# A convolution in nine full taps, and an output projection moved to two later steps, in a two-layer kernel

## The chip, the cores and the metric

One Trainium2 chip, of which the kernel uses one core. The metric is the device time in microseconds (us) of one execution. Each core has a matrix engine (TensorE, PE in the profile), a vector engine (VectorE, DVE), a scalar engine for activation functions (ScalarE, ACT), a general engine (GpSimd, POOL), and a queue (SyncE, SP) that starts transfers. They run side by side, each through its own list of instructions in order, and wait for one another through semaphores.

## The reference, cut to what matters

The input x has 8 images of 128 channels and 128 x 128 points, in float32. Two layers follow each other; the change is in the second alone.

```python
y = conv(x1, conv_w, 3x3, padding 1) + conv_b          # 128 -> 128 channels
seq = y.reshape(B*H*W, 8, 16)                          # each point: 8 tokens of 16
xz = seq @ in_proj.T                                   # to 2 x 32
xi, z = split(xz)
xc = silu(causal conv of 4 over tokens(xi) + b)
dt, Bm, Cm = split(xc @ x_proj.T)                      # 1, 16, 16
dt = softplus(dt * dt_w + dt_b)
h = exp(dt * A) * h + dt * Bm * xc                     # scan over the 8 tokens
ym = (sum over the 16 states of h * Cm) + D * xc
out = (ym * silu(z)) @ out_proj.T
xp = silu(group_norm(out, 4 groups) * gn_w + gn_b)
result = x1 + xp
```

x1 is the output of layer 0 (a dilated convolution, a Fourier stage and a gate), which lies in DRAM.

## The kernel before, in words

Layer 0 ends at about 2950 us and layer 1 fills the rest. Layer 1 goes through 256 blocks, each of 4 rows of one image (512 points): 32 blocks an image, 8 images. Several blocks are in work at once: while block i goes through its scan, block i+3 has its convolution, block i+2 its projection to xc and z, block i+1 its dt, B and C, and block i-1 its last sums and its output projection.

The order is written by hand: under a manual schedule every engine takes its instructions in program order. For each i the program runs `step(i, s)` for s = 2 to 11, and then `seam(i)`. The scan has 16 parts for a block (`s`, 8 tokens by 2 pairs of groups of channels); the names of its operations are:

- `spreads`: TensorE spreads dt*A into the PSUM tile da and dt*xc into ups, for part s+1 and s+2. A tile is 128 partitions x 1024 numbers, made by four matmuls of 16 rows, each shown as two records.
- `exps`: ScalarE takes the exponential of da, in place.
- `inject`: VectorE multiplies ups by B into h. `decay`: VectorE multiplies da by the h of the token before. `add`: VectorE (in parts 4, 7 and 10 GpSimd) adds both.
- `weigh`: GpSimd multiplies h by C into hc. `collect`: TensorE sums hc over the states into the PSUM tile yps. `last_decay`: VectorE, for parts 14 and 15.
- `skip`: TensorE adds D times xc to yps. `ends_sum` and `ends_inputs` begin yps; `gated` multiplies it by silu(z) into ym.
- `project_out`: TensorE projects ym with m_o into the PSUM tile pm, 8 matmuls in two halves of 4; at the end ScalarE copies pm to xr. `keep` later takes the statistics of xr and sends it to DRAM.

[...]da has two buffers (`pair`, shared with `project_x` and `project_z`), ups one, yps one, and pm one. The single pm serves in turn for the convolution, the transpose of its result (`turn`), dt (`project_dt`), B and C (`project_bc`), the output projection, and the sums of the norm. Each use waits until ScalarE has copied the last one out:

```python
    p_u = ctx.enter_context(tc.tile_pool(name="l1_pu", bufs=1, space=PSUM))
    p_a = ctx.enter_context(tc.tile_pool(name="l1_pa", bufs=2, space=PSUM))
    p_m = ctx.enter_context(tc.tile_pool(name="l1_pm", bufs=1, space=PSUM))
    p_y = ctx.enter_context(tc.tile_pool(name="l1_py", bufs=1, space=PSUM))
```

The convolution (`conv`, by `_conv_taps`) is not issued at once but in pieces between the other work: 9 taps, each in two halves of 2 rows (254 or 256 columns), 18 matmuls in all. `CONV` and the `taps` calls of `seam` say how many are issued where. In step 5 `project_bc(i + 1, 1)` is followed at once by the first half of `project_out(i - 1)`; in step 6 the second half and then `skip` follow.

When an image is through, `norm_of` makes its scale and bias, and its 32 blocks are finished one by one beside the next image's: `last_load` (step 8) fetches a block, `last_act` (seam) has ScalarE apply the norm and Silu, `last_sum` (step 9) adds x1 on GpSimd and stores.

In the changed kernel the lines below the first edit stand two lines higher.

Of the kernel before, what the change touches and what calls it, by code (L numbers as in the profile page):

```python
# [116 lines left out]
def _taps(dil):  # L117

    t = [(ky, kx) for ky in range(3) for kx in range(3)]
    t.remove((1, 1))  # L120
    return [(ky * 3 + kx, (ky - 1) * dil, (kx - 1) * dil) for ky, kx in [(1, 1)] + t]


def _conv_taps(nc, outs, wt, srcs, base, r, dil, k0=0, k1=9, parts=1):

    taps = _taps(dil)
    for k in range(k0, k1):
        n, rows = k // parts, 4 // parts  # L130
        t, dy, dx = taps[n]
        a, b = max(0, -(r + dy)), min(4, H - (r + dy))
        a, b = max(a, k % parts * rows), min(b, (k % parts + 1) * rows)
        wa, wb = max(0, -dx), min(W, W - dx)
        for out, src in zip(outs, srcs):
            nc.tensor.matmul(  # L136
                out[:, a:b, wa:wb], wt[:, t, :],
                src[:, r + dy + a - base:r + dy + b - base, wa + dx:wb + dx],
                start=(k == 0), stop=(k == parts * len(taps) - 1), skip_group_check=(parts > 1),
            )  # L140


# [203 lines left out]
def layer1(ctx, tc, x1, w1, c1, out):  # L346
# [12 lines left out]
    nc = tc.nc  # L359
# [5 lines left out]
    wt = const.tile([P, W1_N], F32, name="l1_wt")  # L365
# [7 lines left out]
    def wf(name):  # L373
        at, n = W1[name]
        return wt[:, at:at + n]

    convw = wf("conv_w").rearrange("p (t c) -> p t c", c=C)
# [15 lines left out]
    taps = cf("taps").rearrange("p (k l) -> p k l", l=L)  # L393
    w_k = wf("conv1d_w").rearrange("p (k d) -> p k d", d=DI)
    with tc.tile_pool(name="l1_prep", bufs=2) as prep:
# [18 lines left out]
        for hf in range(NH):  # L414
            for l in range(L):
                k = hf * L + l
# [28 lines left out]
    blocks = [(b, r) for b in range(B) for r in range(0, H, RB)]  # L445
# [6 lines left out]
    def live(i):  # L452
        return 0 <= i < nb
# [13 lines left out]
    def conv(i, k0, k1):  # L467
        d = st8[i]
        if k0 == 0:
            d["pm"] = misc()  # L470
        xin, lo = d["xin"]
        _conv_taps(nc, [d["pm"]], convw, [xin], lo, blocks[i][1], 1, k0, k1, 2)
        if k1 == 18:
            y = wk1.tile([P, RB, W], F32, name="y")
            nc.scalar.activation(y, d["pm"], AF.Identity, bias=wf("conv_b"))
            d["y"] = y
# [40 lines left out]
    def project_bc(i, hf):  # L517
        d, pool = st8[i], wk2 if hf else wk1
        ps = misc().rearrange("p a b -> p (a b)")
        nc.tensor.matmul(ps, m_bcf, d["xc"][:, hf, :], start=True, stop=True)  # L520
        d["bc", hf] = pool.tile([P, N], F32, name=f"bc{hf}")
        nc.scalar.copy(d["bc", hf], ps)  # L522
# [10 lines left out]
    def lay_states(i, hf, k):  # L533

        d, name = st8[i], ("bb", "cc")[k]
        v = wk2.tile([P, LP, N], F32, name=name)
        for lp in range(LP):
            at = (k * LP + lp) * DS
            nc.sync.dma_start(
                v[:, lp, :], d["bc", hf][at:at + DS, :].unsqueeze(1).broadcast_to([DS, 8, N]))  # L540
        d[name, hf] = v
# [76 lines left out]
    def collect(i, t):  # L618

        d = st8[i]  # L620
        for g in range(NG):
            nc.tensor.matmul(  # L622
                d["yps"][g * DI:(g + 1) * DI], gather[:, t % LP, :], d["hc", GP * t + g // GP][:, g % GP],
                start=False, stop=(t in (3, 6)), skip_group_check=True)

    def skip(i, hf):
        d = st8[i]
        nc.tensor.matmul(d["yps"], m_d, d["xc"][:, hf, :], start=False, stop=False, skip_group_check=True)  # L628
# [6 lines left out]
    def project_out(i, k0, k1):  # L635
        d = st8[i]
        if k0 == 0:
            d["pm"] = misc()
        for k in range(k0, k1):
            j, hf = k // NH, k % NH  # L640
            nc.tensor.matmul(  # L641
                d["pm"][:, j, :], d["ym", hf][:, j * C:(j + 1) * C], m_of[:, hf, :],
                start=(hf == 0), stop=(hf == NH - 1))
        if k1 == RB * NH:
            d["xr"] = wk2.tile([P, RB, W], F32, name="xr")
            nc.scalar.copy(d["xr"], d["pm"])
# [33 lines left out]
    fin = {}  # L680
# [9 lines left out]
    def last_act():  # L690
        b, r, sc, bi, v, res = fin["active"] = fin.pop("loaded")
        nc.scalar.activation(v, v, AF.Silu, bias=bi, scale=sc)
# [3 lines left out]
        nc.gpsimd.tensor_add(res, res, v)  # L696
        nc.sync.dma_start(out[b, :, r:r + RB, :], res)

    CONV = {8: (0, 4), 9: (4, 6), 10: (6, 8), 11: (8, 11)}

    def step(i, s):

        now, nxt = live(i), live(i + 1)
        if s == 2:
            if live(i + 4):
                load(i + 4)
            if live(i - 2) and blocks[i - 2][1] + RB == H:
                norm_of(blocks[i - 2][0])
        spreads([(i, s + 1)], [(i, s + 2)])
        exps(i, s + 1)  # L710

        if s == 2:
            if nxt:
                project_dt(i + 1, 0)
            if live(i - 1):
                collect(i - 1, 7)
        elif s == 3:
            if live(i - 1):
                collect(i - 1, 6)
                skip(i - 1, 1)  # L720
            if nxt:
                project_bc(i + 1, 0)
        elif s == 4 and nxt:
            project_dt(i + 1, 1)
        elif s == 5:
            if now:
                ends_sum(i, 0)
            if nxt:
                project_bc(i + 1, 1)
            if live(i - 1):  # L730
                project_out(i - 1, 0, 4)
        elif s == 6:
            if live(i - 1):
                project_out(i - 1, 4, 8)
            if now:
                skip(i, 0)
        elif s == 7 and now:
            collect(i, 1)
        elif s == 9 and now:
            collect(i, 2)  # L740
        elif s == 11 and now:
            collect(i, 3)
        if s in CONV and live(i + 3):
            conv(i + 3, *CONV[s])

        if now:
            decay(i, s)
            if s != 4:
                add(i, s)
            inject(i, s + 2)  # L750
            if s == 5:
                ends_inputs(i, 0)
            if s == 11:
                gated(i, 0)
        if s == 3 and live(i - 1):
            gated(i - 1, 1)

        if now:
            if s == 2:
                end_products(i, 0)  # L760
            else:
                weigh(i, s - 1, (s - 1) // GP)
            if s == 4:
                add(i, s)
            if s == 7:
                end_products(i, 1)
        if s in (3, 4) and nxt:
            inputs(i + 1, s - 3)
        if s == 9 and "active" in fin:
            last_sum()  # L770

        if s == 3 and now:
            lay_states(i, 1, 1)
        elif s == 6 and nxt:
            lay_du(i + 1, 0)
            lay_states(i + 1, 0, 0)
        elif s == 8 and tails:
            last_load()
        elif s == 10 and nxt:
            lay_states(i + 1, 0, 1)  # L780

    def seam(i):


        now, nxt = live(i), live(i + 1)

        def taps(k0, k1):
            if live(i + 3):
                conv(i + 3, k0, k1)

        spreads([(i, 13)], [(i + 1, 0)])
        exps(i, 13)
        if now:
            ends_sum(i, 1)
            decay(i, 12)
            add(i, 12)
            weigh(i, 11, 5)
            weigh(i, 12, 7)
        if nxt:
            lay_states(i + 1, 1, 0)  # L800
        if live(i + 2):
            project_x(i + 2)
        if "loaded" in fin:
            last_act()
        taps(11, 12)
        if now:
            decay(i, 13)
            add(i, 13)
            weigh(i, 13, 7)
        inject(i + 1, 0)  # L810
        if live(i + 2):
            project_z(i + 2)
        spreads([(i, 14)], [(i + 1, 1)])
        exps(i, 14)
        if now:
            ends_inputs(i, 1)
        inject(i + 1, 1)
        taps(12, 15)
        spreads([(i, 15)], [(i + 1, 2)])
        exps(i, 15)  # L820
        if live(i - 1):
            keep(i - 1)
        inject(i + 1, 2)
        if now:
            collect(i, 4)
            last_decay(i, 14)
        taps(15, 18)
        if now:
            weigh(i, 12, 6)
            last_decay(i, 15)  # L830
        spreads([(i + 1, 2)], [(i + 1, 3)])
        exps(i + 1, 2)
        inject(i + 1, 3)
        if now:
            collect(i, 5)
            weigh(i, 13, 6)
        if live(i + 3):
            turn(i + 3)
        if nxt:
            lay_du(i + 1, 1)  # L840
# [95 lines left out]
```

## Time and profile before

The time is 16181.67 us, the median of 3 runs (16174.1 to 16187.9). The profiled execution took 16182.42 us.

| | busy us | share of the span |
|---|---|---|
| TensorE, matmuls | 15146.6 | 94% |
| TensorE, weight loads (beside the matmuls) | 6663.1 | 41% |
| VectorE | 12959.8 | 80% |
| GpSimd | 12024.3 | 74% |
| ScalarE | 8098.5 | 50% |

The page gives, for each group of instructions, the source line, the engine, what it writes and reads, how often it ran, how long it was busy in all and how long one takes; after the last bar stands how long the engine was idle just before it, and what ended most of that idle. In a list of waits each row has the total, the number and the longest. A row of windows has, for a stretch of time, the busy time of each engine, then the clock that TensorE was granted (1.00 is full speed), the share of the transfer engines and GB/s. In a timeline each row has the start, the time, the engine, the line and the operation, the number of instructions merged, and in brackets the idle before.

TensorE's mean granted clock in this execution is 0.967.

### The profile page before, as it was taken

What the parts mean: (1) busy time and instruction counts of PE and PEld (TensorE: products, weight loads), DVE (VectorE), ACT (ScalarE), POOL (GpSimd) and SP (SyncE); (2) the same over time, 40 slices, a digit from 0 to 9 for tenths busy, and PEclk for the clock granted to TensorE, in tenths of its full rate; (3) what the DMA queues carried; (4) which work ended last, traced back from release to release, by engine and by line L of the source; (5) the groups of instructions that cost most, each with busy time, mean ns of one, the idle gap of its engine ahead of it and who ended that gap; (6) DMA issues with size and microseconds to landing.
All of it is one profiled execution on the core that took longest, in us unless ns stands there. A gap on an engine that the chain in (4) does not pass through costs nothing.

```text
span 16180.6 us, 210804 instructions
## 1 busy us (share of the span) xinstructions
PE 15146.6 (94%) x76456; PEld 6663.1 (41%) x76456; DVE 12959.8 (80%) x13691; ACT 8098.5 (50%) x8726; POOL 12024.3 (74%) x5892
## 2 busy tenths in 40 slices
PE   9989898999999999999999999999999999999996
PEld 4546455533333333333333333333333343333332
DVE  1515233799989999999999999999999999999995
ACT  1222212455555555555555555555555555555553
POOL 0101101588889898898898988988899889888996
PEclk9999999999999999999999999999999999999997
DMA  2322222465566666666666666666666666666665
GB/s 77 86 78 76 74 72 79 100 117 114 117 119 132 132 132 131 128 134 129 131 132 129 134 127 132 130 131 129 131 131 131 132 131 131 130 130 130 132 134 134
DMA packets 1075791, 1933.19 MB, mean 119 GB/s; under 512 B 123968, under 2 KB 255040, under 8 KB 1058368
## 3 DMA queue, kind: packets, MB, share of 16 engines
q1 hardware_dynamic: 1001472, 1850.17, 53.7%
q10 hardware_dynamic: 73280, 69.54, 1.5%
q8 instruction: 607, 9.95, 0.2%
q14 instruction: 432, 3.54, 0.1%
HBM read 375.71 MB, written 201.33 MB: 36 GB/s over the span
## 4 chain that ended last, share of the span: by engine, by line
PE 65%; DVE 14%; issue 8%; ACT 8%; POOL 3%; DMA 2%; SPq 0%; ACTq 0%; DVEq 0%; POOLq 0%
PE da L556 16%; PE yps L622 8%; PE pm L136 7%; PE cps L136 6%; PE pm L641 4%; DVE h L571 4%; DVE da L587 4%; PE yps L628 3%; PE ups L556 3%; PE da L492 3%; ACT da L561 3%; DVE h L595 2%; ACT L561 2%; DVE hc L606 2%; PE pm L508 2%
## 5 line engine op out<-in xcount | busy, mean ns | idle before, releaser
L601 POOL TENSOR_TENSOR hc<-h,cc 128x1024 f32<-128x1024 f32 x3584 | 8366.3, 2361 | 608.3 <-DVE h L595 572.7
L561 ACT ACTIVATE da<-da 128x1024 f32<-128x1024 f32 x3584 | 3612.6, 1008 | 4299.9 <-PE ups L556 2359.3
L571 DVE TENSOR_TENSOR h<-ups,bb 128x1024 f32<-128x1024 f32 x3584 | 4370.6, 1219 | 1037.2 <-PE ups L556 768.3
L556 PE MATMUL da<-du,m_a 16*128 16x512 f32 x14336 | 4145.1, 655 | 30.6 <-DVE hc L606 6.6
L556 PE MATMUL ups<-du,m_u 16*128 16x512 f32 x14336 | 4168.7, 654 | 0.7 <-DVE h L571 0.7
L595 DVE TENSOR_TENSOR h<-da,h 128x1024 f32<-128x1024 f32 x2304 | 2821.3, 1225 | 79.1
L587 DVE TENSOR_TENSOR da<-da,h 128x1024 f32<-128x1024 f32 x2304 | 2819.6, 1224 | 4.8 <-issue 1.1
L136 PE MATMUL pm<-xin,l_wt 128*128 128x254 f32 (+2 forms) x9216 | 2444.3, 398 | 5.9 <-DMA l_wt<-w 4.5
L593 POOL TENSOR_TENSOR h<-ah,h 128x1024 f32<-128x1024 f32 x768 | 1812.2, 2360 | 649.1 <-DVE ah L585 571.4
L136 PEld LDWEIGHTS pm<-xin,l_wt 128*128 128x128 f32 x9216 | 1637.9, 191 | 1501.6 <-issue 1353.7
L622 PE MATMUL yps<-hc,l_ct 128*32 128x512 f32 x14336 | 1945.6, 615 | 1.3 <-POOL hc L601 1.2
L556 PEld LDWEIGHTS da<-du,m_a 16*128 16x128 f32 x14336 | 1085.2, 185 | 1919.0 <-issue 968.2
L274 POOL TENSOR_TENSOR xr<-xr,sq 128x512 f32<-128x512 f32 x128 | 160.4, 1265 | 1654.8 <-ACT sq L273 1614.8
L556 PEld LDWEIGHTS ups<-du,m_u 16*128 16x128 f32 x14336 | 1105.7, 185 | 198.0 <-DVE h L571 122.5
L641 PE MATMUL pm<-m_o,ym 128*128 128x128 f32 x4096 | 715.3, 328 | 382.8 <-ACT bc L522 382.2
L136 PE MATMUL cps<-xin,l_wt 128*64 128x500 f32 (+2 forms) x4608 | 1024.5, 583 | 38.7 <-issue 30.3
L224 DVE COPY fT<-tps 128x512 f32<-128x512 f32 x128 | 88.5, 692 | 1180.0 <-PE tps L223 1180.0
L561 ACT ACT_TABLE_LOAD x774 | 993.0, 1283 | 16.8 <-PE ups L556 0.7
L641 PEld LDWEIGHTS pm<-m_o,ym 128*128 128x128 f32 x4096 | 604.4, 227 | 836.8 <-ACT bc L522 592.5
L585 DVE TENSOR_TENSOR ah<-da,h 128x1024 f32<-128x1024 f32 x768 | 932.4, 1214 | 0.0
L340 POOL TENSOR_TENSOR og<-og,xg 128x512 f32<-128x512 f32 x128 | 164.3, 1284 | 968.5 <-ACT og L339 831.7
L622 PEld LDWEIGHTS yps<-hc,l_ct 128*32 128x32 f32 x14336 | 284.3, 108 | 1392.0 <-issue 1054.2
(150 smaller groups left out, 15907.7 us busy)
## 6 DMA issues: line engine op xcount, KB each, us to landing
bb<-bc SPq DMA_DIRECT2D x2048, 256.0 KB
cc<-bc SPq DMA_DIRECT2D x2048, 256.0 KB
du<-dt SPq DMA_DIRECT2D x2048, 64.0 KB
du<-u SPq DMA_DIRECT2D x2048, 64.0 KB
xin<-x SPq DMA_DIRECT2D x112, 640.0 KB
xin<-x SPq DMA_DIRECT2D x48, 1408.0 KB
gn<-xr SPq DMA_DIRECT2D x256, 256.0 KB
v<-gn SPq DMA_DIRECT2D x256, 256.0 KB
```

What stands on the lines that cost most here:

```text
L136: nc.tensor.matmul(out[:, a:b, wa:wb], wt[:, t, :], src[:, r + dy + a - base:r + dy + b - base, wa + dx:wb + dx], start=(k == 0), stop=(k ...
L492: nc.tensor.matmul(ps[:, hf], m_xh[:, hf, :], d["yT"], start=True, stop=True)
L556: nc.tensor.matmul(o, w, v, start=True, stop=True)
L561: nc.scalar.activation(da, da, AF.Exp)
L571: nc.vector.tensor_mul(h, d["ups", s], state_row(i, "bb", s // GP))
L585: nc.vector.tensor_mul(d["ah"], da, before)
L587: nc.vector.tensor_mul(da, da, before)
L593: nc.gpsimd.tensor_add(h, d["ah"], h)
L595: nc.vector.tensor_add(h, d["da", s], h)
L601: nc.gpsimd.tensor_mul(hc, d["h", s], state_row(i, "cc", t))
L622: nc.tensor.matmul(d["yps"][g * DI:(g + 1) * DI], gather[:, t % LP, :], d["hc", GP * t + g // GP][:, g % GP], start=False, stop=(t in (3, ...
L641: nc.tensor.matmul(d["pm"][:, j, :], d["ym", hf][:, j * C:(j + 1) * C], m_of[:, hf, :], start=(hf == 0), stop=(hf == NH - 1))
```

## The change

Three edits, all in layer 1:

1. The convolution is issued as 9 full taps of 4 rows (508 or 512 columns) instead of 18 halves. Before, steps 8, 9, 10, 11 had 2, 1, 1 and 1.5 taps and the three places of the seam 0.5, 1.5 and 1.5; now the steps have 1, 1, 1 and 2, and the seam 1, 2 and 1. The seam's first group stands ahead of `project_x` instead of behind it.
2. `skip` (D times x) comes first in step 6. The first half of the output projection goes from step 5 to step 6, behind it; the second half from step 6 to step 8, ahead of the convolution's first tap. Nothing stands any more between B and C's projection in step 5 and the spreads of step 6.
3. In the seam, `last_act` (the norm's Silu) comes ahead of `project_x` and so ahead of the Silu of xc.

They are meant to shorten TensorE's waits for pm and for da, and to halve the convolution's instructions. The instructions of VectorE, GpSimd and the transfer queue stay in their order; ScalarE's copy of xr comes two exponentials later. The core of the diff:

```diff
-def _conv_taps(nc, outs, wt, srcs, base, r, dil, k0=0, k1=9, parts=1):
+def _conv_taps(nc, outs, wt, srcs, base, r, dil, k0=0, k1=9):
...
-    for k in range(k0, k1):
-        n, rows = k // parts, 4 // parts
+    for n in range(k0, k1):
         t, dy, dx = taps[n]
         a, b = max(0, -(r + dy)), min(4, H - (r + dy))
-        a, b = max(a, k % parts * rows), min(b, (k % parts + 1) * rows)
...
-                start=(k == 0), stop=(k == parts * len(taps) - 1), skip_group_check=(parts > 1),
+                start=(n == 0), stop=(n == len(taps) - 1),
...
-    CONV = {8: (0, 4), 9: (4, 6), 10: (6, 8), 11: (8, 11)}
+    CONV = {8: (0, 1), 9: (1, 2), 10: (2, 3), 11: (3, 5)}
...
             if nxt:
                 project_bc(i + 1, 1)
+        elif s == 6:
+            if now:
+                skip(i, 0)
             if live(i - 1):
                 project_out(i - 1, 0, 4)
-        elif s == 6:
-            if live(i - 1):
-                project_out(i - 1, 4, 8)
-            if now:
-                skip(i, 0)
         elif s == 7 and now:
             collect(i, 1)
+        elif s == 8 and live(i - 1):
+            project_out(i - 1, 4, 8)
         elif s == 9 and now:
             collect(i, 2)
...
             lay_states(i + 1, 1, 0)
+        taps(5, 6)
+        if "loaded" in fin:
+            last_act()
         if live(i + 2):
             project_x(i + 2)
-        if "loaded" in fin:
-            last_act()
-        taps(11, 12)
...
-        taps(12, 15)
+        taps(6, 8)
...
-        taps(15, 18)
+        taps(8, 9)
```

More of the change, by code (lines that the diff above doesn't have):

```diff
@@ L471, in conv @@
         xin, lo = d["xin"]
-        _conv_taps(nc, [d["pm"]], convw, [xin], lo, blocks[i][1], 1, k0, k1, 2)
-        if k1 == 18:
+        _conv_taps(nc, [d["pm"]], convw, [xin], lo, blocks[i][1], 1, k0, k1)
+        if k1 == 9:
             y = wk1.tile([P, RB, W], F32, name="y")
```

## The prediction

> **What bounds the kernel now.** I read the page first, then the waits, then steady-state windows, then one block's timeline.
>
> The page's busy line and the list of waits:
>
> ```profile
> PE 15146.6 (94%) x76456; PEld 6663.1 (41%) x76456; DVE 12959.8 (80%) x13691; ACT 8098.5 (50%) x8726; POOL 12024.3 (74%) x5892
> ```
>
> ```profile
> PE pm L641 <- ACT bc L522: 382.2, 254, 1.5
> ...
> PE da L492 <- DVE h L595: 188.4, 253, 0.7
> ```
>
> TensorE (PE) is fullest, and two waits strike it once in each of the 256 blocks: 1.50 us before the output projection (L641), which wants the single PSUM buffer pm while ScalarE still copies bc out of it, and 0.75 us before x's projection (L492).
>
> The windows: two whole blocks, then 3.4 us slices around the 1.50 us wait in the slow block (three slices) and in the fast one (three):
>
> ```profile
> 8906.70:8956.35 49.65, 47.25 (x249) 19.42 (x248) 46.51 (x43) 28.86 (x30) 45.68 (x23) 1.00 0.67 142
> 10026.00:10077.30 51.30, 48.90 (x253) 20.43 (x248) 46.54 (x43) 28.89 (x31) 45.27 (x23) 0.97 0.64 135
> 10036.10:10039.50 3.40, 3.40 (x13) 1.27 (x12) 3.37 (x4) 3.35 (x4) 2.88 (x2) 1.00 0.03 8
> 10039.50:10042.90 3.40, 1.90 (x13) 1.28 (x16) 3.36 (x4) 1.80 (x3) 3.40 (x3) 1.00 0.00 0
> 10042.90:10046.30 3.40, 3.40 (x17) 2.21 (x10) 2.58 (x3) 1.15 (x2) 1.55 (x1) 0.51 0.05 19
> 8916.50:8919.90 3.40, 3.40 (x18) 1.21 (x18) 3.40 (x4) 2.44 (x3) 3.02 (x2) 1.00 0.91 158
> 8919.90:8923.30 3.40, 2.50 (x10) 0.67 (x4) 3.37 (x4) 3.36 (x5) 2.88 (x3) 1.00 0.17 25
> 8923.30:8926.70 3.40, 2.79 (x21) 1.91 (x22) 3.04 (x4) 1.08 (x3) 3.40 (x2) 1.00 0.00 0
> ```
>
> Blocks come in kinds. The fast one takes 49.65 us at clock 1.00. In the slow one, the slice holding the whole wait has PE busy only 1.90 of 3.40 us, and the next slice runs at half clock (0.51). In the fast block the same wait is cut by the edge of two slices (2.50 and 2.79 busy) and the clock stays. ScalarE's y (L475) starts from 3204.4 to 15877.7, 250 times: 12673.3/249 = 50.90 us per block on average. So half clock costs 50.90 - 49.65 = 1.25 us a block, and the wait itself comes on top.
>
> The fast block's TensorE, ScalarE and VectorE timelines at the places that matter:
>
> ```profile
> 8921.38 1.02 PE L520 MATMUL pm<-xc,m_bc 128*128 128x512 f32 x2
> 8923.91 1.16 PE L641 MATMUL pm<-m_o,ym 128*128 128x128 f32 x8 [1.50 <-ACT bc L522]
> ...
> 8926.07 1.16 PE L641 MATMUL pm<-m_o,ym 128*128 128x128 f32 x8
> 8927.06 1.02 PE L628 MATMUL yps<-xc,m_d 128*128 128x512 f32 x2
> ...
> 8931.61 1.99 PE L136 MATMUL pm<-xin,l_wt 128*128 128x256 f32 x8
> ...
> 8946.65 1.98 PE L492 MATMUL da<-yT,m_x 128*128 128x512 f32 x4 [0.75 <-DVE h L595]
> 8948.47 0.59 PE L136 MATMUL pm<-xin,l_wt 128*128 128x254 f32 x2
> ```
>
> ```profile
> 8922.34 1.01 ACT L561 ACTIVATE da<-da 128x1024 f32<-128x1024 f32 x1
> 8923.26 0.59 ACT L522 COPY bc<-pm 128x512 f32<-128x512 f32 x1
> ```
>
> ```profile
> 8926.26 1.23 DVE L571 TENSOR_TENSOR h<-ups,bb 128x1024 f32<-128x1024 f32 x1 [0.31 <-PE ups L556]
> 8929.28 1.23 DVE L571 TENSOR_TENSOR h<-ups,bb 128x1024 f32<-128x1024 f32 x1 [0.67 <-PE ups L556]
> ```
>
> VectorE is busy 46.51 of 49.65 us and idles in two places: 0.31 + 0.67 us just after PE's 1.50 us wait, and 0.80 + 0.73 + 0.16 us in the seam. Elsewhere it runs without gaps (one of 0.15), so PE's time counts only where VectorE then waits for ups. GpSimd (45.68 busy) idles the other 4.0 us and is not the limit.
>
> [...]
>
> **The change, part by part.** PE times are from the fast block, 8900 taken off.
>
> Nine full taps for eighteen half taps. A float32 matmul shows as two records. Eight half-tap records take 8933.53 - 8931.61 = 1.92 us, six take 1.48, so each further one costs 0.22 or less, against a 0.19 us weight load beside it: the loads are hidden already. A full 512-column record steps at 0.43 us (the two of L628), twice that. So 36 x 0.213 = 18 x 0.427 = 7.7 us a block: gain 0, though half the instructions go. The groups stay seven; what changes is their size: step 8 loses a tap (-0.85), step 11 gains half (+0.43), the seam has 1 + 2 + 1 taps for 0.5 + 1.5 + 1.5.
>
> Output projection out of step 5. After bc (L520, from 21.38) PE goes straight to step 6. Its da buffer is free since 21.7 (VectorE's add of step 5), its ups buffer when inject(7) ends at 22.84. So the spreads run 22.34 to 23.94, D times x 23.94 to 24.9, then L641's first half to 25.9; bc's copy ended at 23.85, so pm is free. The ups for step 8 are done at 24.0 and VectorE's inject(8) starts at 25.86, back to back, instead of 26.26; the ups for 9 follow at 28.2, and inject(9) starts at about 28.25 instead of 29.28. VectorE gains **1.03 us** here and both idle gaps are gone.
>
> Second half in step 8, a new wait. The convolution's first tap needs pm, which ScalarE must first copy into xr. PE: spreads to 30.55, L641 (8 records, 1.05) to 31.6. ScalarE's exp ends at 31.3, so the copy runs from 31.74 for 0.585 and the tap starts at about 32.37: PE idles 0.8 us (bounds: 0.6 with no hand-over time, 1.5 as for bc now). Queued behind are one tap (1.06) and step 9's spreads, ready at 34.5; VectorE wants them at 35.3. The idle is hidden, with 0.8 us to spare, because step 8 has one tap less.
>
> Seam. add(12) is done 1.03 earlier, at 45.55. PE: ends_sum to 45.1, the new tap to 46.07 (it fills what was the 0.75 wait), x's projection to 47.9, z's to 49.15, spreads 50.3. Before, spreads ended at 51.30: 1.0 kept. Two taps instead of one and a half then take 0.43: inject(2) of the next block is 0.7 earlier. The last group is 0.43 shorter but PE must wait for last_decay(14), on VectorE, so next block's first spreads start at 55.78 against 56.49. Kept: **0.71 us a block**. The Silu of the norm now fills ScalarE's 1.53 us wait for L492; z's Silu starts when PE gives it, and the exp after it has slack: 0.
>
> Clock. The largest PE idle left inside one 3.4 us window is the 0.8 us of step 8; the slices with 2.50 and 2.79 us busy (0.6 to 0.9 idle) did not lose the clock. So the half-rate slices go: **1.25 us a block** saved.
>
> Sum: 0.71 + 1.25 = 1.96 us a block, 48.94 a block. From block 3 to 255 (253 blocks): 1.96 x 253 = 496 us, 16182 - 496 = 15686. Layer 0 and the tail are untouched.
>
> **The rivals.**
> - Forecast, 48.9 us a block: 15686. Chance 0.62.
> - Clock kept, but the new step-8 wait or the longer seam group takes back the 0.71. For: the new wait stands in a stretch (steps 8 to 11) where VectorE has no gaps, so any ups that comes late costs at once. Against: the 0.8 us of spare. 16182 - 1.25 x 253 = 15866. Chance 0.15.
> - Half rate stays, brought on by the idle in step 8, next to spreads that PE does piecemeal while waiting for VectorE. Against: 0.8 us is little over half of 1.50. 16182 - 0.71 x 253 = 16002. Chance 0.10.
> - Better: the spreads' waits for VectorE shrink too, VectorE nears its 46.5 plus one gap of 1.5: 48.0 to 48.3 a block, about 15520. Chance 0.06.
> - Slower: each block now meets a half-rate window, where at present about half do, at 15 x 3.413 = 51.2 a block: 16182 + 0.3 x 253 = 16258. For: today's slow blocks hold 51.27, so that the wait meets the same place of the next window. Against: the long wait is gone, and 48.94 plus 1.6 = 50.5 would not lock in. Chance 0.07.
>
> **How the numbers follow.** The predicted time is the first case. The range from 15510 to 15950 takes in the first, second and fourth (0.83), and with them a hand schedule off by 0.3 us a block or so, and the new wait's upper bound of 1.5 us (0.7 beyond the 0.8, less than the spare); the third and fifth (0.17) are left out. Faster by over 0.2%: the first four less some of the third's upper side, 0.91; same: 0.02; slower 0.07.
>
> **What would show it.** Right: PE's wait of L641 for bc gone; a wait of about 0.8 us of the convolution for the xr copy in step 8; no wait of L492 for VectorE; PEclk near 1.00 from 3000 to 15900; no idle of VectorE after step 5; about 48.9 us between starts of y; the convolution's records half as many and twice as long, its total busy time the same. Wrong: PEclk staying at 0.97, a step-8 wait over 1.6 us, or VectorE idling longer in the seam than 1.7 us.

## The result, and the profile after

The changed kernel takes 15807.6 us (median of 4 runs, 15803.33 to 15808.82), the one before in the same comparison 16184.78 us. The ratio is 0.9766, 95% interval 0.975 to 0.9783: 377 us, 2.3% faster. The forecast was 15686 us, a gain of 496 us; the result lies inside its range.

The page's busy line and two of its groups, and from the list of waits the one that the change brought:

```profile
PE 15002.4 (95%) x71848; PEld 5732.8 (36%) x71848; DVE 12932.0 (82%) x13691; ACT 8126.9 (51%) x8726; POOL 12028.2 (76%) x5892
...
L569 DVE TENSOR_TENSOR h<-ups,bb 128x1024 f32<-128x1024 f32 x3584 | 4364.3, 1218 | 688.1 <-PE ups L554 307.2
...
L134 PE MATMUL pm<-xin,l_wt 128*128 128x508 f32 (+1 forms) x4608 | 2409.4, 623 | 176.0 <-ACT xr L644 170.2
```

```profile
PE pm L134 <- ACT xr L644: 170.2, 252, 0.7
```

The waits of 382.2 us (output projection for bc) and 188.4 us (x's projection for VectorE) are gone from the list. In place of the first stands the convolution's wait for the copy into xr, 0.7 us in each block. The second was not saved but moved: TensorE still waits for VectorE in the seam, now ahead of spreads (L554) and of z's projection (L499), for 134.6 + 76.0 = 210.6 us in all.

```profile
PE da L554 <- DVE hc L604: 134.6, 255, 1.5
...
PE da L499 <- DVE h L593: 76.0, 253, 0.5
```

The convolution has half the records and each takes longer, with 2409.4 us busy in all against 2444.3. VectorE's idle before the product with ups fell from 1037.2 to 688.1 us.

Windows of the changed kernel: one whole block, the 3.4 us slice with the new wait, the slice after it, and then nearly all of layer 1 (columns as before; the one after the POOL count is the clock):

```profile
8879.10:8928.32 49.22, 47.73 (x233) 16.31 (x233) 46.42 (x43) 29.00 (x31) 45.72 (x23) 1.00 0.63 131
8901.40:8904.80 3.40, 2.72 (x21) 1.59 (x17) 3.37 (x4) 1.60 (x2) 3.40 (x2) 1.00 0.81 90
8904.80:8908.20 3.40, 3.40 (x19) 1.04 (x20) 3.37 (x4) 1.01 (x1) 3.40 (x3) 1.00 0.91 203
```

```profile
4500.00:15400.00 10900.00, 10555.74 (x50777) 3609.56 (x50776) 10258.11 (x9331) 6412.43 (x6634) 10082.38 (x4851) 1.00 0.64 135
```

The slice with the wait has PE busy 2.72 of 3.40 us, and the next one keeps clock 1.00; so does layer 1 as a whole. Nearly the same stretch of the kernel before, 4500 to 15800, stood at 0.97. The 49.65, 51.27 and longer blocks have, but for those about the end of an image, become one kind: 49.22 us. The start of y runs from 3199.9 to 15495.3 us, 250 times, which makes 12295.4/249 = 49.38 us a block on average, against 50.90.

The changed kernel's timelines at the same places, TensorE first, then VectorE's idle times in one block:

```profile
8902.94 1.16 PE L639 MATMUL pm<-m_o,ym 128*128 128x128 f32 x8
8904.78 1.12 PE L134 MATMUL pm<-xin,l_wt 128*128 128x512 f32 x2 [0.68 <-ACT xr L644]
...
8920.53 1.13 PE L499 MATMUL da<-yT,m_z 64*128 64x512 f32 x4 [0.30 <-DVE h L593]
```

```profile
8880.32 1.23 DVE L569 TENSOR_TENSOR h<-ups,bb 128x1024 f32<-128x1024 f32 x1 [0.16 <-PE ups L554]
8900.60 1.22 DVE L569 TENSOR_TENSOR h<-ups,bb 128x1024 f32<-128x1024 f32 x1 [0.16 <-PE ups L554]
8910.24 1.22 DVE L569 TENSOR_TENSOR h<-ups,bb 128x1024 f32<-128x1024 f32 x1 [0.22 <-issue]
8922.92 1.22 DVE L569 TENSOR_TENSOR h<-ups,bb 128x1024 f32<-128x1024 f32 x1 [0.80 <-PE ups L554]
8925.90 1.22 DVE L569 TENSOR_TENSOR h<-ups,bb 128x1024 f32<-128x1024 f32 x1 [1.15 <-issue]
```

The kernel before, in step 10 and in the seam:

```profile
8938.84 1.23 DVE L571 TENSOR_TENSOR h<-ups,bb 128x1024 f32<-128x1024 f32 x1 [0.15 <-issue]
8951.52 1.22 DVE L571 TENSOR_TENSOR h<-ups,bb 128x1024 f32<-128x1024 f32 x1 [0.80 <-PE ups L556]
8954.08 1.22 DVE L571 TENSOR_TENSOR h<-ups,bb 128x1024 f32<-128x1024 f32 x1 [0.73 <-issue]
```

Read down these brackets of after against those of before. After step 5 VectorE idled 0.31 + 0.67 us; now 0.16. In step 10 it was 0.15; now 0.22. In the seam it was 0.80 + 0.73; now 0.80 + 1.15. So 0.8 us is won behind step 5, and half of it is lost in the seam before the third product of the next block (8925.90), which follows the middle group of taps.

### The profile page after: what moved, and what is told of

Its sections match the earlier page's. It is cut to its first block, busy times and chain, and to the rows that moved or that the text cites. A ratio compares the mean times of both kernels' runs of the same rounds, so it can differ in the third digit from the quotient of the medians.

```text
span 15801.5 us, 201588 instructions
## 1 busy us (share of the span) xinstructions
PE 15002.4 (95%) x71848; PEld 5732.8 (36%) x71848; DVE 12932.0 (82%) x13691; ACT 8126.9 (51%) x8726; POOL 12028.2 (76%) x5892
## 4 chain that ended last, share of the span: by engine, by line
PE 71%; DVE 17%; issue 5%; ACT 4%; DMA 2%; POOL 1%; SPq 0%; ACTq 0%; DVEq 0%; POOLq 0%
PE da L554 18%; PE yps L620 8%; PE ups L554 7%; PE pm L134 7%; PE cps L134 6%; DVE da L585 6%; DVE h L593 4%; DVE h L569 4%; PE yps L626 3%; PE pm L506 3%; PE pm L639 3%; PE pm L518 3%; DVE hc L604 2%; PE da L499 2%; PE yps L610 2%
## 5 line engine op out<-in xcount | busy, mean ns | idle before, releaser
L569 DVE TENSOR_TENSOR h<-ups,bb 128x1024 f32<-128x1024 f32 x3584 | 4364.3, 1218 | 688.1 <-PE ups L554 307.2
L554 PE MATMUL da<-du,m_a 16*128 16x512 f32 x14336 | 4070.9, 644 | 139.1 <-DVE hc L604 134.6
L554 PE MATMUL ups<-du,m_u 16*128 16x512 f32 x14336 | 4117.5, 643 | 1.9 <-DVE h L569 1.3
L134 PE MATMUL pm<-xin,l_wt 128*128 128x508 f32 (+1 forms) x4608 | 2409.4, 623 | 176.0 <-ACT xr L644 170.2
L554 PEld LDWEIGHTS da<-du,m_a 16*128 16x128 f32 x14336 | 1080.2, 184 | 2623.3 <-issue 1010.3
L134 PEld LDWEIGHTS pm<-xin,l_wt 128*128 128x128 f32 x4608 | 750.5, 189 | 1617.3 <-issue 1392.3
L554 PEld LDWEIGHTS ups<-du,m_u 16*128 16x128 f32 x14336 | 1125.3, 184 | 378.9 <-DVE h L569 297.2
L513 POOL TENSOR_TENSOR u<-dt,xc 128x512 f32<-128x512 f32 x512 | 652.7, 1275 | 169.8 <-ACT dt L508 169.8
L218 ACT ACTIVATE feat<-cps,bn_t,bn_s 128x512 f32<-128x512 f32 x128 | 99.5, 778 | 1224.1 <-PE cps L134 1224.1
```

Of the source, the lines that this page charges most:

```text
L134: nc.tensor.matmul(out[:, a:b, wa:wb], wt[:, t, :], src[:, r + dy + a - base:r + dy + b - base, wa + dx:wb + dx], start=(n == 0), stop=(n ...
L513: nc.gpsimd.tensor_mul(d["u", hf], d["dt", hf], d["xc"][:, hf, :])
L554: nc.tensor.matmul(o, w, v, start=True, stop=True)
L569: nc.vector.tensor_mul(h, d["ups", s], state_row(i, "bb", s // GP))
```

## The experiments

Times are medians; ratios are to the kernel before, with 95% intervals. Mean block times are worked out from the starts of y as above; a steady block is the commonest distance between two such starts.

**1. The size of a tap.** The changed kernel with halves again, in the same places.

```diff
-        _conv_taps(nc, [d["pm"]], convw, [xin], lo, blocks[i][1], 1, k0, k1)
+        _conv_taps(nc, [d["pm"]], convw, [xin], lo, blocks[i][1], 1, 2 * k0, 2 * k1, 2)
```

> The changed kernel with each tap cut again into two halves of two rows, in the same places. Theory (weight loads are hidden, so the size of a tap is worth nothing): 15808 us within 0.2% (15776 to 15840), a steady block of 49.2 us, TensorE's clock as in the changed kernel. Rival (half as many convolution instructions is where the gain comes from): back towards 16185, 16100 or more.

15814.02 us, ratio 0.9783 (0.9768 to 0.9798), beside 0.9766 for the changed kernel: the intervals overlap. 4608 matmul records (2304 matmuls) and as many weight loads more cost nothing that can be measured. The size of the taps is worth nothing; their new places are another matter (experiment 11).

**2 and 3. The projection's move alone, and all but that.** Edit 2 on the kernel before; and the changed kernel without edit 2.

```diff
+        elif s == 6:
+            if now:
+                skip(i, 0)
             if live(i - 1):
                 project_out(i - 1, 0, 4)
-        elif s == 6:
-            if live(i - 1):
-                project_out(i - 1, 4, 8)
-            if now:
-                skip(i, 0)
...
+        elif s == 8 and live(i - 1):
+            project_out(i - 1, 4, 8)
```

> The kernel before with the second edit alone: D times x first in step 6, the output projection's halves in steps 6 and 8; the convolution stays in half taps in its old places, the norm's Silu stays behind. Theory (the gain is the wait of 1.5 us taken out of step 5, with the half clock it brings): nearly all of the gain or more, 15720 to 15830 us, half-rate slices gone, a steady block of 49.0 to 49.3 us. If step 8, which keeps two taps behind the new wait, has no room for them, VectorE idles there and the block is 49.6, 15900. Rival (the seam's edit or the full taps bring the gain): 16100 or more.

> The changed kernel with the output projection and D times x back in steps 5 and 6: full taps, their new places and the norm's Silu ahead stay. Theory: the 1.5 us wait and the half-rate slices stay, mean clock about 0.967 again, and the seam's edit alone is worth nothing or costs a little: 16150 to 16300 us. Rival (the seam's edit or the full taps bring the gain): 15800 to 15950.

Edit 2 alone: 15899.99 us, 0.9834 (0.9818 to 0.9851), not what the theory had but what it gave for the case that step 8 has no room. Without it: 16631.65 us, 1.0286 (1.0271 to 1.0301), slower than before and further off than was expected. Layer 1 with edit 2 alone, and then without it:

```profile
4500.00:15500.00 11000.00, 10637.73 (x54743) 4362.57 (x54740) 10280.70 (x9331) 6364.61 (x6636) 10084.28 (x4852) 1.00 0.65 133
```

```profile
4500.00:15500.00 11000.00, 10469.91 (x48040) 3427.22 (x48042) 9747.50 (x8830) 6090.32 (x6282) 9532.96 (x4585) 0.94 0.61 126
```

The move alone gives the clock back (1.00), and its steady block is 49.7 us: no shorter than the fast block of before. The other edits alone lengthen the fast block to 50.1 us, and the clock is down to 0.94. The 1.50 us wait is still there, but most of the half clock does not follow it. In the trace of the kernel before, the 123 halvings of the clock between 4000 and 15300 us, and their ends, lie on a grid of 3.413 us, to within 0.004 us; 103 of them last one such window, and 96 come 51.2 us after the one before, which is 15 windows and about the length of the slow block (51.27). Here are two such windows of the kernel before that hold the wait (but for 0.07 us of it in the second), each with the next one:

```profile
9169.13:9172.54 3.41, 1.91 (x7) 0.75 (x6) 3.40 (x4) 2.96 (x4) 3.17 (x2) 1.00 0.00 0
9172.54:9175.95 3.41, 3.41 (x26) 2.10 (x24) 3.06 (x4) 1.44 (x2) 2.72 (x2) 1.00 0.02 9
9988.33:9991.75 3.42, 1.98 (x16) 1.28 (x16) 3.38 (x4) 1.38 (x2) 3.42 (x2) 1.00 0.03 5
9991.75:9995.16 3.41, 3.41 (x14) 2.21 (x10) 2.41 (x3) 1.59 (x2) 1.59 (x2) 0.50 0.11 43
```

And three of the kernel without edit 2 (the wait; the window that loses the clock; the one after it), with what TensorE does in the first two:

```profile
8948.24:8951.65 3.41, 1.91 (x9) 0.96 (x8) 3.05 (x4) 2.73 (x3) 3.41 (x2) 1.00 0.00 0
8958.48:8961.89 3.41, 3.19 (x12) 0.90 (x10) 3.38 (x4) 1.55 (x2) 3.41 (x3) 1.00 0.73 86
8961.89:8965.31 3.42, 3.42 (x13) 0.70 (x10) 3.38 (x4) 0.37 (x1) 3.42 (x2) 0.50 0.97 187
```

```profile
8948.51 1.02 PE L518 MATMUL pm<-xc,m_bc 128*128 128x512 f32 x2
8951.03 1.16 PE L639 MATMUL pm<-m_o,ym 128*128 128x128 f32 x8 [1.50 <-ACT bc L520]
...
8958.74 1.13 PE L134 MATMUL pm<-xin,l_wt 128*128 128x512 f32 x2
8960.08 1.13 PE L554 MATMUL da<-du,m_a 16*128 16x512 f32 x4 [0.21 <-DVE h L593]
8961.21 1.45 PE L554 MATMUL ups<-du,m_u 16*128 16x512 f32 x4
```

Between 4000 and 15300 us, the kernel before has 184 windows at full clock in which TensorE idles 1.2 to 1.7 us, and 123 of them are followed by half clock. Without edit 2 it is 11 of 136; there 122 of 133 halvings follow a window with less than 0.7 us of idle, like the one at 8958.48, which has a tap and spreads in it. So idle time is not all that counts; the last section comes back to this.

VectorE's idle with edit 2 alone, in steps 8 to 10:

```profile
8902.86 1.23 DVE L571 TENSOR_TENSOR h<-ups,bb 128x1024 f32<-128x1024 f32 x1 [0.17 <-PE ups L556]
8906.05 1.22 DVE L571 TENSOR_TENSOR h<-ups,bb 128x1024 f32<-128x1024 f32 x1 [0.83 <-POOL hc L601]
```

What VectorE gained behind step 5 it gives back here: step 8 has the new wait and two taps behind it. The view puts the second idle down to GpSimd, whose product ended at 8906.01; but the last spreads for this line start at 8905.30 and take 0.59, and with the wait gone and two taps still in step 8 (experiment 11) this idle is 0.15.

**4 and 5. The new wait made longer.** The copy out of pm is made two and three times.

```diff
             nc.scalar.copy(d["xr"], d["pm"])
+            nc.scalar.copy(d["xr"], d["pm"])
```

> The changed kernel in which ScalarE copies the projected block out of pm twice (the same values to the same place), so that the convolution's first tap in step 8 waits 0.6 us longer, about 1.3 us. Theory: about 0.7 us of this wait's aftermath is spare, so 0.6 more costs little (0 to 0.2 us a block, 15800 to 15860 us), and 1.3 us idle is at the edge of what halves the clock; mean clock 0.98 or more if it stays under. Rival (the new wait is already on the path, with no spare): +0.59 x 253 = 15957.

> The changed kernel with the copy out of pm made three times, so that the convolution's first tap in step 8 waits about 1.9 us instead of 0.7. Theory (a wait of 1.5 us or more inside one 3.4 us window halves TensorE's clock): half-rate slices come back, mean clock 0.97 or less; with those (some 1.2 us a block or more) and 0.5 us past the spare, 16100 to 16350 us. Rival (the half clock before had another cause than the wait): clock stays 0.986 and only the wait past the spare counts, 15900 to 15960.

16241.47 us, 1.0046 (1.0031 to 1.0061), and 17211.33 us, 1.0645 (1.062 to 1.067). The convolution's wait in the list of waits, and layer 1, first with two copies, then with three:

```profile
PE pm L134 <- ACT xr L645: 326.3, 252, 1.3
```

```profile
4500.00:15500.00 11000.00, 10533.18 (x49431) 3562.76 (x49430) 9998.60 (x9082) 6368.32 (x6673) 9815.90 (x4720) 0.97 0.64 130
```

```profile
PE pm L134 <- ACT xr L646: 481.5, 252, 1.9
```

```profile
4500.00:15500.00 11000.00, 10456.68 (x45837) 3433.63 (x45835) 9305.34 (x8429) 6025.84 (x6390) 9113.75 (x4376) 0.91 0.61 120
```

0.6 us more of waiting costs 434 us, 1.2 us more costs 1404 us. Both expectations were too low, and so were both rivals. The half clock comes back in part at a wait of 1.3 us already (mean clock 0.97), and there is more of it at 1.9 us (0.91). And nothing was spare: with two copies the steady block is 49.86 us, 0.64 more than 49.22, about as much as a copy takes (0.59 us).

**6 and 7. The wait avoided, and a tap moved.** The projection's second half in step 7, so that the copy runs beside step 8's spreads; then, besides, one tap from the seam's middle group to step 8.

```diff
-        elif s == 7 and now:
-            collect(i, 1)
-        elif s == 8 and live(i - 1):
-            project_out(i - 1, 4, 8)
+        elif s == 7:
+            if now:
+                collect(i, 1)
+            if live(i - 1):
+                project_out(i - 1, 4, 8)
```

```diff
-    CONV = {8: (0, 1), 9: (1, 2), 10: (2, 3), 11: (3, 5)}
+    CONV = {8: (0, 2), 9: (2, 3), 10: (3, 4), 11: (4, 6)}
...
-        taps(5, 6)
+        taps(6, 7)
...
-        taps(6, 8)
+        taps(7, 8)
```

> The changed kernel with the output projection's second half in step 7, behind the sums there, instead of step 8. The copy to xr then runs beside step 8's spreads. Theory: the 0.7 us wait of the first tap is gone, but it was hidden, so the time stays within 0.3%: 15760 to 15850. Rival (the wait was on the path): 0.7 us a block less, 15640.

> As the last, and one tap taken out of the seam's middle group and put into step 8 (2, 1, 1, 2 taps in steps 8 to 11, then 1, 1, 1). Theory (the middle group of two taps delays the next block's third product by 0.43 us more than before, which is what the changed kernel fell short by): VectorE's idle in the seam shrinks by 0.4 to 0.8 us a block, 15600 to 15710 us. Rival (the seam is set by VectorE's own chain or by GpSimd): 15760 to 15850.

15794.89 us, 0.9775 (0.9759 to 0.9792): without the wait the time is the same, so the 0.7 us were hidden, just. With the tap moved, 15663.71 us, **0.9693 (0.9679 to 0.9708)**, the fastest of all (experiment 11 comes within its interval). VectorE's idle in its seam:

```profile
8905.78 1.22 DVE L569 TENSOR_TENSOR h<-ups,bb 128x1024 f32<-128x1024 f32 x1 [0.80 <-PE ups L554]
8908.29 1.23 DVE L569 TENSOR_TENSOR h<-ups,bb 128x1024 f32<-128x1024 f32 x1 [0.69 <-issue]
```

The 1.15 us before the third product is 0.69, and the steady block is 48.7 us.

**8. The norm's Silu.** Put behind that of xc again.

```diff
-        if "loaded" in fin:
-            last_act()
         if live(i + 2):
             project_x(i + 2)
+        if "loaded" in fin:
+            last_act()
```

> The changed kernel with the norm's Silu behind that of xc again. Theory (ScalarE has slack there, the third edit is worth nothing or close to it): 15790 to 15840 us. Rival (z's Silu behind three others frees da late): 0.3 us a block more, 15880.

15800.91 us, 0.9779 (0.9764 to 0.9793): the third edit is worth nothing.

**9 and 10. Idle filled with work of no use.** In the kernel before, a matmul whose result nobody reads is put into the 1.50 us wait. In the kernel with two copies, a matmul with a matrix of zeros is put into the 1.3 us wait and added to yps.

```diff
                 project_bc(i + 1, 1)
+            if now:
+                idle = p_u.tile([P, GP, N], F32, name="ups")
+                nc.tensor.matmul(idle[:, 0], m_d, st8[i]["xc"][:, 0, :], start=True, stop=True)
             if live(i - 1):
                 project_out(i - 1, 0, 4)
```

```diff
             project_out(i - 1, 4, 8)
+            if now:
+                nc.tensor.matmul(
+                    st8[i]["yps"], m_zero, st8[i]["xc"][:, 0, :], start=False, stop=False, skip_group_check=True)
```

> The kernel before with one matmul of no use added in its wait: after B and C's projection in step 5 TensorE writes D times xc (two records of 0.43 us) into the ups buffer, which is free once the product of part 7 is done and is overwritten by the next spreads. Theory (what costs 1.25 us a block is the halved clock, and it comes from TensorE's idle within one 3.4 us window): the idle falls to about 0.6 us, the clock stays, mean 0.985 or so, the block stays at 49.65 to 49.8 us throughout, 15860 to 15920 us: faster by added work. Rival (the wait costs as a wait, the clock is a by-stander): no change or slower, 16160 or more.

> The changed kernel with two copies out of pm, and in the lengthened wait of step 8 a matmul with a matrix of zeros that is added to yps (two records, 0.95 us). The wait of the convolution for pm stays as long; TensorE is only busy in part of it. Theory (two copies cost 433 us of which some 0.65 us a block, 165 us, is the wait and the rest the halved clock): 15950 to 16000 us, clock 0.985, a steady block of 49.9 us. Rival: 16240 as with two copies alone.

15908.47 us, 0.9838 (0.9822 to 0.9855), and 15944.68 us, 0.986 (0.9845 to 0.9875). TensorE's timeline in the first of them, and its layer 1:

```profile
8932.80 1.02 PE L520 MATMUL pm<-xc,m_bc 128*128 128x512 f32 x2
8934.31 1.13 PE L732 MATMUL ups<-xc,m_d 128*128 128x512 f32 x2 [0.49 <-DVE h L571]
8935.33 1.16 PE L641 MATMUL pm<-m_o,ym 128*128 128x128 f32 x8
```

```profile
4500.00:15500.00 11000.00, 10678.88 (x55217) 4355.35 (x55216) 10281.96 (x9333) 6386.63 (x6638) 10085.67 (x4853) 1.00 0.63 133
```

The output projection starts as late as before: 8935.33 - 8932.80 = 2.53 us behind bc's first matmul, as 8923.91 - 8921.38 = 2.53 did. The wait is as long and work is added, and the kernel is 1.6% faster: TensorE's idle in it is down to 0.49 us, and its clock stays at 1.00. With two copies the useless matmul brings 16241 down to 15945, just under what was expected; what is left over the changed kernel, 137 us or 0.54 a block, is the price of the longer wait as such. Both useless matmuls use 128 rows and 128 columns of the array.

**11. The projection moved, and nothing else, to steps 6 and 7.** The kernel before with its half taps in their old places, and of the change only the projection and D times x, the second half behind the sums of step 7.

> The kernel before with only the output projection moved, its halves to steps 6 and 7, and D times x first in step 6: half taps in their old places, 2 of them's worth in step 8, the seam untouched. Theory (moving the projection alone left VectorE no gain because step 8 had the new wait and two taps; without the wait there the 0.9 us that VectorE gains after step 5 reaches the next block, as the seam's middle group is no longer than before): a steady block of 48.7 to 48.9 us, 15650 to 15720 us, as with the tap moved out of the seam. Rival (the seam's own edit is needed for the gain to reach the next block): 49.4 to 49.7 us a block, 15850 to 15900.

15678.67 us, 0.9702 (0.9686 to 0.9719), a steady block of 48.7 us. This part of the change, placed one step earlier, brings 3.0%, more than the whole change; the edits of the taps, the seam and the Silu aren't needed for it. This kernel differs from that of experiment 6 in edits 1 and 3 alone, and its block is shorter, 48.75 us against 49.17. As the size of the taps and the Silu are worth nothing (experiments 1 and 8), it is the new places of the taps that cost about 0.4 us a block.

## Why the prediction was right, and where it was off

- **The 1.50 us wait as the thing to remove: right.** It is gone, and edit 2 alone (experiment 2) removes it. In the kernel before, the copy out of pm started at 8923.26, 0.86 us after bc's matmuls ended (8922.40): ScalarE had two table loads (ACT_TABLE_LOAD) of 1.28 us ahead of it, at 8919.05 and 8921.05.
- **The half clock as the larger half of the gain: right, and shown; idle alone does not account for it.** Experiments 4, 5, 9 and 10 set the idle and the wait apart. A longer wait brings the half clock back, and filling the idle with useless work takes it away, with the wait unchanged. The size was 1.25 us a block, from mean less fast block. It measures less: the changed kernel's mean is still 49.38 - 49.22 = 0.16 us over its steady block, for blocks at the end of an image (53 to 57 us, once an image) that both kernels have. So about 1.1 of the 1.25 was the clock's; experiment 9 alone brings (16172.78 - 15908.47)/253 = 1.04. But the prediction judged a window by TensorE's idle alone, and held 1.50 us to be enough. It is not always: 61 of the 184 such windows before kept the clock, and in experiment 3 windows with little idle lost it. The changed kernel happens to have hardly any of that other kind (7 halvings in all between 4000 and 15300 us). The prediction did not look for them, so that they are few is luck.
- **Full taps worth nothing: right** (experiment 1). **The norm's Silu worth nothing: right** (experiment 8).
- **VectorE's gain of 1.03 us behind step 5: nearly right.** The brackets give 0.98 - 0.16 = 0.82 there, less 0.07 in step 10.
- **The seam, "Kept: 0.71 us a block": the term that was mis-sized.** It measures 49.65 - 49.22 = 0.43. For the product behind the middle group the working had 1.0 us less 0.43 us for the longer group, which leaves 0.57 and not the 0.7 that was written down; the 0.71 itself was read one group later, at the next block's first spreads. By the brackets, 0.82 us is won, 0.07 lost in step 10 and 1.15 - 0.73 = 0.42 lost in the seam, which leaves 0.33; VectorE is also busy 0.09 us less. Experiment 7 takes the tap out of that group, and the idle there falls from 1.15 to 0.69 us and the block to 48.7.
- **The new wait of 0.8 us (0.6 to 1.5), hidden with 0.8 to spare: the wait right, the spare wrong.** It measures 0.68 us and is hidden (experiment 6). But the spare was read at the product of step 9 alone; the next one, in step 10, waits for its ups already (0.22 us; its last spreads end at 8910.09, it starts at 8910.24), so any further delay counts in full, as experiments 4 and 10 show (0.64 and 0.54 us a block for a copy of 0.59). The upper bound of 1.5 us would have been dear in two ways, by its length and by the clock: waits of 1.3 and 1.9 us cost 434 and 1404 us more (experiments 4 and 5).

In sum, of the 1.96 us a block forecast, 50.90 - 49.38 = 1.52 came: 0.28 less in the seam, and 0.16 less from the image ends. 1.52 x 253 = 385 us, against 377 measured.

The rival that the half rate stays, brought on by the idle of step 8, failed for this kernel, but by a smaller margin than it was given: with a wait 0.6 us longer the mean clock is 0.97 (experiment 4).

## What to carry to other kernels

When a matrix engine is nearly full, look at its clock beside each wait: here waits of 1.5 us (before) and 1.3 us (two copies) cost 1.0 to 1.2 us a block in half speed (experiments 9 and 10), and as waits 0.9 (experiment 11) and 0.5 to 0.6. Find the windows that lose the clock and look at what is in them, idle or not. If the wait there can't be removed, it can be filled; splitting it was not tried. And when a second use of a single buffer is moved, put enough other work between the copy out and the next use, and check the spare at every consumer behind it, not at the first alone.

## What the runs showed that was not expected

- A matmul that computes nothing of use made the kernel before 1.6% faster (experiment 9), about 260 us.
- The wait of step 8 leaves the clock alone at 0.68 us (mean 1.00); at 1.3 us the mean is 0.97, at 1.9 us 0.91.
- The same wait of 1.50 us stands in the kernel before (mean clock 0.97) and in the one without edit 2 (0.94, experiment 3), where most halvings come elsewhere. What else the window holds differs with the outcome. Of the 184 windows before with 1.2 to 1.7 us of idle, the 61 that kept the clock have at most 0.29 us of spreads in them, 0.07 on average (records of spreads use 16 of the array's 128 rows). Of the 123 that lost it, 121 have more than 0.3 us, and the average is 0.65. The mean idle is 1.50 us in the one kind and 1.49 in the other.
- So it is in the windows shown under experiments 2 and 3: no spreads in those that kept the clock (9169.13, 8948.24), 0.89 us (9988.33) and 2.1 us (8958.48) in those that lost it. No run changed the spreads alone; that they cause it was not shown.
